# A graph attention layer on one Trainium2 core: block products and spread loads in batch 0, a store queue more in the tail, setup matmuls of 32 outputs

## The chip, the cores and the metric

The kernel runs on one core of one Trainium2 chip. The metric is the device time of one execution, in microseconds (us). Three executions of the kernel before took 587.0, 587.73 and 588.74 us; the median is 587.73. One more execution was recorded by the hardware profiler, and everything said of the inside of the kernel comes from that one. Engines go by their profile names: PE (TensorE matmul) and PEld (its weight loads), DVE (VectorE), ACT (ScalarE), POOL (GpSimd), SP (SyncE, which here only issues DMAs).

## The reference, cut to what matters

There are B = 16 batches of N = 512 tokens with F = 512 features (`v`, in the kernel `x`), one condition vector `q` per batch, and an integer mask `adj` of 11 labels per pair of tokens. Only the first 20 tokens (`NONGT`) serve as keys and values. Heads: 16 of 32 features. Everything is float32.

```
row_zero  = v.sum(-1) == 0
q_exp     = where(row_zero, 0, q)                      # per token
self_feat = concat([v, q_exp]) @ W_self.T + b_self
output    = self_feat
for d in range(2):                                     # two directions
    A    = (adj if d == 0 else adj^T)[:, :, :20]
    cond = A.sum(-1);  vb = A @ w_bias + b_bias
    kv   = self_feat[:, :20]
    qh, kh = self_feat @ Wq[d].T + bq[d], kv @ Wk[d].T + bk[d]      # 16 heads of 32
    aff  = where(cond > 0, qh . kh / sqrt(32), NEG) + vb
    out_t  = softmax(aff over the 20 keys) @ kv
    output = output + out_t @ Wout[d] + bout[d]
result = v + relu(output)
```

## The kernel before, in words

**Weights folded into the keys.** The queries are never computed. In a setup, for all 16 batches at once, the kernel forms the 20 key and value rows of each batch (`ps_kv`, L530 to L573: 16 matmuls of 128 outputs, `kv_terms`), the key rows kh (`key_rows`, L576: 32 matmuls of 128 outputs by 320 columns, L580), and multiplies them with Wq, so that a score is self_feat times one "g" column per head and key. This last step are 22 key bursts (`keys`, L659): a burst of matmuls (L668) into two pairs of banks, evicted by ACT (L683) and DVE (L685) into a stage `st`, which SP writes to DRAM (g1_d for batch 1, g_d for the later ones, L693 and L694) or copies to g0 for batch 0 (L690). While ACT and DVE evict a burst, PE is given other work by a plan written out by hand: `plan` (L713) has one word for each burst from the one at which the key rows are done, and each letter takes the next step of its kind: b biases, c bias scores, n row flags (ps_nz), v and w the values kv times Wout (ps_v, L643), s a quarter (8 matmuls) of half a block of self features.

**Self features.** For one batch, self_feat is a 512 x 512 by 512 x 492 product (the 20 key tokens come from the setup). Batch 0 computes it directly, in four blocks of 32 matmuls (ps_sf, L205, each of 32 outputs; four of them, on the four quarters of the array's columns, make one step). Three blocks are in the plan, the fourth stands in the loop at b = 0, nt = 1 (L867). Each is evicted by two DVE instructions (`self_copy`, L218). The later batches use seven products of half-size blocks instead of eight: sums of the weight blocks (`weight_sums`, L223) and of the x blocks (`x_sum`, L238) are made by POOL, each product (`product`, L249) is 16 matmuls of 32 outputs by 246 columns (L282) into the banks ps_a (two, kept accumulating through products 1, 6, 7 and 4), ps_d (product 2) and ps_c (5, then 3 on top), and DVE takes `partial` sums out of ps_a (L289) between products and adds them to ps_d and ps_c (`joined`, L299). A product on ps_a must wait until the partial before it has been read.

**The loop.** It runs over b (16 batches) and nt (4 tiles of 128 tokens); the order of every instruction is fixed by the program's text. In each step: `scores` (ps_s, L356, 128 matmul records), `weigh` on DVE (add the mask terms `full`, maximum, subtract: L370, L374, L378), `expo` on ACT (L383), `normal` of the previous tile (DVE sum and reciprocal L409 and L410, POOL multiply L411), `turn` (DVE transpose, L418). The products for batch b + 1 stand at nt = 2 (1, 2), nt = 3 (6, 7, 5), and at nt = 0, b + 1 (4, 3). `attend(b - 1)` (ps_o, L429) stands at nt = 2 of batch b: it multiplies the softmax weights with `vd`, a tile of value blocks; then `finish` (L438, L440), `residual` (POOL, L443) and `store` (L448). Mask terms of the next batch: `mask_mul` (ACT, L317), `mask_count`, `mask_sum` (DVE, L328), `mask_spread` (ACT, L337), `full_add` (POOL, L344). Row sums of x, which say where the q term is left out, are taken by ACT two batches ahead (`row_sum`, L169, from `xn`), turned into flags (`row_mask`) and loaded back over DRAM (`load_nz`).

**Value blocks.** bd_d in DRAM holds the values of all batches as blocks among zeros. SP clears it with one DMA of 2 MB (`clear_blocks`, L145) at b = 0, nt = 1, then copies the values vw_d into it with 12 DMAs from DRAM to DRAM (`blocks`, L162) at nt = 2, which wait for the clear. `load_values(b)` (L139) reads one batch of it into vd with four DMAs, which wait for the copies; for batch 0 this stands at nt = 3, ahead of the loads of x(2).

**Queues.** All loads and stores of the loop are issued by SP, in the order of the text. `behind(dma, ins)` (L95) gives a DMA a wait for an instruction of another engine, so that it isn't issued too early; SP then stands still until that instruction is done.

**The tail.** After the loop (L980 to L1014): `attend` of the last batch in two parts (three tiles, one tile), with the self features put into the banks by matmuls; `end` (DVE maximum, L996), a relu by ACT (L1006) with an add by POOL (L1009), and `send` (L998), four stores, all on SP. Just ahead, the last tile's softmax is done in two halves (`weigh_half`, `normal_half`, L385 and L396; L400 is the multiply, for the second half on DVE).

## Time and profile before

| What | Value |
|---|---|
| times of three executions | 587.0, 587.73, 588.74 us (median 587.73) |
| the profiled execution | 589.14 us, its span 587.3 us |
| granted TensorE clock in it | 0.995 |
| first key burst, first scores of batch 0 | 25.44 us, 91.15 us |
| first attend (batch 0's, in batch 1) | 132.13 us |
| batches 5 to 14 | 262 to 555 us |
| last DVE `end` done | 581.6 us |

The span is the time from the first to the last event that the profiler saw; the 1.8 us beside it are around the program. A row of a timeline gives start and length in us, the engine, the line of the kernel, the operation, the tile written and the tiles read, the shape, and the count in the group; brackets say how long the engine had been idle and what released it. The chain of waits follows the last instruction back, at each step to what released it or to the instruction before it on its engine; in order of time its rows are start, length and what it was. A float32 matmul appears as two records, so counts of PE records are twice those of the program.

### The profile page before, as it was taken

To read this page: it belongs to the slowest core of one execution; us is meant where nothing else is said; L and a number is where in the kernel's file an instruction comes from. 1 tells how busy PE (TensorE), PEld (TensorE's weight loads), DVE (VectorE), ACT (ScalarE), POOL (GpSimd) and SP (SyncE) were. 2 spreads that over 40 slices of the span, in tenths; PEclk is the share of its full clock that TensorE was granted. 3 is DMA by queue.
4 is the path that set the end of the run, shared out by engine and by line. 5 is a ranking of instruction groups with operands and counts; after the bars stand their busy time and mean duration, and the time that the engine had idled before them with its cause. 6 is when DMAs were issued, how large, how long until landed. Compare 5 with 4: busy or idle time off the path is not lost.

```text
span 587.3 us, 30302 instructions
## 1 busy us (share of the span) xinstructions
PE 575.0 (98%) x13180; PEld 436.8 (74%) x13180; DVE 491.2 (84%) x785; ACT 395.5 (67%) x1162; POOL 384.3 (65%) x351
## 2 busy tenths in 40 slices
PE   9999999999999999999999999999999999999993
PEld 6654547887778787877778787787878878787881
DVE  1485565889898989899999999998989898989895
ACT  1334534686877777878686868686877868776761
POOL 2406663548677685858586867776868686777774
PEclk9999999999999999999999999999999999999998
DMA  8999899857766675757676767675666766664403
GB/s 312 387 400 314 330 376 333 256 110 209 231 179 188 188 211 169 216 172 214 173 201 180 217 169 210 175 210 167 198 196 188 210 187 182 210 171 136 121 31 127
DMA packets 103221, 124.14 MB, mean 211 GB/s; under 512 B 21713, under 2 KB 71921, under 8 KB 101041
## 3 DMA queue, kind: packets, MB, share of 16 engines
q1 hardware_dynamic: 101840, 120.32, 66.3%
q8 instruction: 104, 1.70, 1.2%
q0 software_dynamic: 672, 1.36, 1.0%
q10 hardware_dynamic: 576, 0.53, 0.3%
q14 instruction: 29, 0.23, 0.1%
HBM read 82.30 MB, written 40.24 MB: 209 GB/s over the span
## 4 chain that ended last, share of the span: by engine, by line
PE 94%; DVE 3%; DMA 1%; issue 1%; ACT 0%; POOL 0%; SPq 0%; DVEq 0%; POOLq 0%; ACTq 0%
PE ps_s L356 44%; PE ps_a L282 17%; PE ps_c L282 9%; PE ps_o L429 6%; PE ps_d L282 4%; PE ps_v L643 3%; PE ps_k L580 3%; PE ps_sf L205 2%; DMA ws_q<-in_wsT 1%; PE ps_kv L531 1%; DVE o L438 0%; PE ps_nz L189 0%; DVE wt L418 0%; DVE ps_s L374 0%; DVE sm L409 0%
## 5 line engine op out<-in xcount | busy, mean ns | idle before, releaser
L356 PEld LDWEIGHTS ps_s<-g,sf 128*32 128x32 f32 x8192 | 263.3, 110 | 20.1 <-issue 12.2
L356 PE MATMUL ps_s<-g,sf 128*32 128x152 f32 x8192 | 276.7, 293 | 0.5 <-ACT st L683 0.5
L337 ACT COPY both<-add 32x80 f32<-32x80 f32 x512 | 130.9, 256 | 53.6 <-DVE add L328 47.6
L411 POOL TENSOR_TENSOR s<-s,sm 128x640 f32<-128x640 f32 x63 | 80.3, 1275 | 95.5 <-DVE sm L410 54.7
L344 POOL TENSOR_TENSOR full<-cq,both 128x640 f32<-128x640 f32 x64 | 100.2, 1565 | 28.5 <-issue 22.6
L317 ACT ACTIVATE prod<-adj,wb_sb 128x80 f32<-128x80 int32 x330 | 112.5, 432 | 0.8 <-DMA adj<-in_adj 0.8
L383 ACT ACTIVATE s<-s 128x640 f32<-128x640 f32 x63 | 46.5, 738 | 65.6 <-DVE s L378 65.3
L443 POOL TENSOR_TENSOR o<-o,x 128x512 f32<-128x512 f32 x60 | 76.0, 1288 | 0.0
L370 DVE TENSOR_TENSOR full<-ps_s,full 128x608 f32<-128x608 f32 x63 | 48.9, 777 | 29.7 <-PE ps_s L356 24.4
L409 DVE TENSOR_REDUCE sm<-s 128x32 f32<-128x640 f32 x63 | 50.9, 807 | 9.2 <-ACT s L383 8.9
L282 PE MATMUL ps_a<-t,ws_s 128*32 128x246 f32 x960 | 55.4, 370 | 0.0
L374 DVE TENSOR_REDUCE ps_s<-full 128x32 f32<-128x640 f32 x63 | 52.2, 828 | 2.2
L418 DVE STREAM_TRANSPOSE wt<-s 128x640 f32<-128x640 f32 x63 | 52.8, 839 | 0.1
L378 DVE TENSOR_TENSOR s<-full,ps_s 128x640 f32<-128x640 f32 x63 | 51.5, 818 | 1.1
L282 PEld LDWEIGHTS ps_a<-t,ws_s 128*32 128x32 f32 x960 | 31.5, 110 | 16.1
L328 DVE TENSOR_REDUCE add<-prod 128x80 f32<-128x960 f32 x32 | 36.8, 1150 | 6.1 <-ACT prod L317 4.3
L247 POOL TENSOR_TENSOR t<-x 128x492 f32<-128x492 f32 x30 | 34.4, 1148 | 10.2 <-DVE full L370 5.3
L429 PE MATMUL ps_o<-wt,vd 32*32 32x512 f32 (+5 forms) x816 | 37.8, 578 | 2.3 <-DVE wt L403 2.0
L440 ACT ACTIVATE o<-o,bo 128x512 f32<-128x512 f32 x60 | 38.3, 711 | 0.6 <-POOL biased L888 0.6
L438 DVE TENSOR_TENSOR o<-ps_o,sf 128x512 f32<-128x512 f32 x60 | 36.7, 668 | 0.0
L289 DVE SCALAR_TENSOR_TENSOR u<-nz,qw,ps_a 128x246 f32<-128x246 f32 x90 | 36.6, 449 | 0.0
L247 POOL TENSOR_TENSOR t<-x,t 128x492 f32<-128x492 f32 x30 | 34.4, 1147 | 1.9 <-DMA x<-in_xT 0.7
(238 smaller groups left out, 719.6 us busy)
## 6 DMA issues: line engine op xcount, KB each, us to landing
g_d<-st SPq DMA_DIRECT2D x16, 1064.0 KB, 5.8
g<-g_d SPq DMA_DIRECT2D x56, 304.0 KB, 3.6
out_T<-o SPq DMA_DIRECT2D x60, 256.0 KB, 3.5
x<-in_xT SPq DMA_DIRECT2D x56, 256.0 KB, 3.3
xn<-in_xn SPq DMA_DIRECT2D x52, 256.0 KB, 3.2
adj<-in_adj SPq DMA_DIRECT2D x56, 220.0 KB, 3.3
nz<-nz_d SPq DMA_DIRECT2D x14, 256.0 KB, 4.3
wk<-in_wkT SPq DMA_DIRECT2D x2, 1024.0 KB, 7.6
```

The source lines that it names most:

```text
L247: done["xsum"] = nc.gpsimd.tensor_sub(t, one, two)
L282: nc.tensor.matmul(to, lhs, x[:, k], start=start, stop=stop, skip_group_check=n != 2)
L317: nc.scalar.activation(p[:, :, l], a[:, :, l], AF.Identity, scale=wb_sb[:, l : l + 1])
L337: nc.scalar.copy(adds[b, h][bass.ts(a, R), :, g], add[r].rearrange("p (t m) -> p t m", t=2))
L344: done["full"] = nc.gpsimd.tensor_add(f, cqs[b].unsqueeze(1).to_broadcast(shape), adds[b, nt // 2][:, nt % 2].unsqueeze(2).to_broadcast(sh ...
L356: nc.tensor.matmul(bank[bass.ts(a, R), bass.ts(j, WD // HL)], sfs[b][:, k, bass.ds(nt * P + (2 * g + j) * R, R)], keys[:, k, a], start=(k ...
L374: nc.vector.tensor_reduce(mx, f, AX.X, ALU.max)
L378: done["weigh"] = nc.vector.tensor_sub(s, f, mx.unsqueeze(3).to_broadcast(full))
L411: done["normal"] = nc.gpsimd.tensor_mul(s, s, sm.unsqueeze(3).to_broadcast(full))
L418: nc.vector.transpose(wts[b][:, nt], s.rearrange("p a h m -> p (a h m)"))
L429: nc.tensor.matmul(banks[a][bass.ds(at // 2 * DH, n * DH)].rearrange("p (t n) -> p t n", n=32), vd[r, bass.ds(at * DH, n * DH)], wt[r, :, ...
L443: nc.gpsimd.tensor_add(o[:, c], o[:, c], xs[b][:, c])
```

## The change

Five things, told by the new program:

1. Batch 0 computes its self features by the seven products too. They are steps "p" of the plan, in the gaps of the last bursts, each with its partial or join on DVE right behind; nothing of it is left in the loop. The weight sums and the x sums of batch 0 (kept in a free slot of the self feature pool) are made by POOL at bursts 9 and 11. The values come earlier in the plan, the bursts 12 and 13 (counted from 0) have only a "w" behind them.
2. For all batches, `partial` writes into the block of self features itself and `joined` adds in place; the tile is made, and its first 20 columns are copied in, at nt = 2 rather than 3.
3. Loads in batch 0 are spread. The clear is eight DMAs of 256 KB, each behind an instruction of the loop, the last behind the POOL add `full_add(0, 2)`. The keys of batch 1 come in four parts, the masks of batch 1 in halves. `blocks()` stands after batch 1's last mask load and has 18 DMAs: its 12 copies and between them two key loads and four loads of xn(2). `load_values(0)` goes from b = 0, nt = 3 to b = 1, nt = 0, behind a `joined`, after the four loads of x(2). `row_sum(2)` goes to b = 1, nt = 0, on ACT ahead of that tile's mask spread and exponential, and `row_mask(2)` follows it.
4. In the tail, the POOL adds wait for the last multiply of the softmax (`done["half"]`), and two of the four stores are issued by ACT's queue.
5. In the setup, `kv_terms` and `key_rows` issue four matmuls of 32 outputs for each one of 128.

The diff, cut to its core:

```diff
-    def clear_blocks(zero):
-        nc.sync.dma_start(
-            bd_d.rearrange("c b r e i g -> (c b r) (e i g)").rearrange("(n p) w -> p n w", p=P),
-            zero.unsqueeze(1).to_broadcast([P, C * B * 32 // P, HL * 2 * DH]),
-        )
+    def clear_blocks(zero, n, ins):
+        half = bd_d[n // 2, n % 2 * (B // 2) : (n % 2 + 1) * (B // 2)]
+        behind(nc.sync.dma_start(
+            half.rearrange("b r e i g -> (b r) (e i g)").rearrange("(n p) w -> p n w", p=P),
+            zero.unsqueeze(1).to_broadcast([P, B * 16 // P, HL * 2 * DH]),
+        ), ins)
...
-                        nc.sync.dma_start(bb[:, r : r + hi - lo, e, i], vv[d, :, m : m + hi - lo, e])
+                        copies.append((bb[:, r : r + hi - lo, e, i], vv[d, :, m : m + hi - lo, e]))
+        for n, (to, of) in enumerate(copies):
+            nc.sync.dma_start(to, of)
+            if n in (2, 5):
+                load_keys(1, range(n // 3 + 2, n // 3 + 3))
+            if n in (7, 8, 9, 10):
+                load_xn(2, (n - 7) // 2, None, slice((n - 7) % 2, (n - 7) % 2 + 1))
...
-    def partial(b, n, f, l, to=None):
-        if to is None:
-            to = us[b, n] = xsum.tile([P, 2, HN], F32, tag=f"u{n}", name=f"u{b}_{n}")
+    def partial(b, f, l):
+        to = block(b, f, l)
...
             def kv_terms(fc, k):
-                nc.tensor.matmul(
-                    kv_ps[fc][:, :BM], ws_v[:, k, bass.ts(fc, P)], xkv[:, k],
-                    start=(k == 0), stop=(k == C - 1),
-                )
+                for a in range(HL):
+                    nc.tensor.matmul(
+                        kv_ps[fc][bass.ts(a, R), :BM], ws_v[:, k, bass.ds(fc * P + a * R, R)], xkv[:, k],
+                        start=(k == 0), stop=(k == C - 1),
+                    )
...
+            def block_product(n):
+                product(0, n)
+                f, args = {
+                    1: (partial, (0, 0, 0)), 2: (joined, (0, "d", 0, 0)), 6: (partial, (0, 0, 1)),
+                    7: (partial, (0, 1, 1)), 5: (joined, (0, "c", 1, 1)), 4: (partial, (0, 1, 0)),
+                    3: (joined, (0, "c", 0, 1)),
+                }[n]
+                f(*args)
...
-            plan = "bvv vv vv ccw vv ns ssss sssw vv vv ssss ssss vv vv nww ssss ssss".split()
+            plan = "bvv vvc vvc vvn vv vvw vv vv w w wn p p p p p p p".split()
...
+                if n == 9:
+                    row_sums(1)
+                    weight_sums()
                 if n == 11:
-                    row_sums(1)
-                if n == 13:
-                    weight_sums()
+                    new_self(0)
+                    for i in range(1, 5):
+                        x_sum(0, i)
...
                 if b == 0 and nt == 1:
-                    load_adj(1, 0)
-                    load_cq(1)
-                    clear_blocks(zero)
-                    load_adj(1, 1)
-                    load_xn(2, 0)
-                    load_xn(2, 1)
-                if b == 0 and nt == 2:
-                    blocks()
-                if nt == 2 and last or nt == 3 and b == 0:
+                    clear_blocks(zero, 2, done["xsum"])
+                if nt == 2 and last:
                     load_values(b)
...
                         mask_mul(b, 1)
+                        if b == 1:
+                            for j in range(4):
+                                row_sum(2, j)
                         product(b, 4)
...
-                        joined(b, 3, "c", 1, 1)
+                        joined(b, "c", 1, 1)
                         product(b, 3)
-                        if b > 1:
-                            load_values(b - 1, done["joined"])
+                        load_values(b - 1, done["joined"])
...
-                    if b == 0:
-                        self_feat(0, 1, 1)
...
                     full_add(b, 2)
+                    if b == 0:
+                        clear_blocks(zero, 7, done["full"])
...
-                    if b > 0 and more:
+                    if b == 0:
+                        load_keys(1, range(1, 2), done["sum"])
+                        load_adj(1, 1, done["normal"], slice(0, 1))
+                        load_adj(1, 1, None, slice(1, 2))
+                        blocks()
+                    elif more:
                         load_keys(b + 1, range(1), done["normal"])
...
-        send(0, 0, NT - 1)
+        send(nc.sync, 0, 0, NT - 1)
...
-            nc.gpsimd.tensor_add(o_last[:, n, ns], o_last[:, n, ns], xs[b][:, n, ns])
-        send(2, 0, NT - 1)
+            behind(nc.gpsimd.tensor_add(o_last[:, n, ns], o_last[:, n, ns], xs[b][:, n, ns]), done["half"])
+        send(nc.scalar, 2, 0, NT - 1)
         for q in range(4):
             end(NT - 1, NT, rest, q)
             if q % 2:
-                send(q - 1, NT - 1, NT)
+                send(nc.scalar if q == 1 else nc.sync, q - 1, NT - 1, NT)
```

`key_rows` is changed as `kv_terms` is; the other seven calls of `clear_blocks` stand at nt = 0 and 1 of batch 0.

114 lines of the change are left out of this document (53 added, 61 removed).

## The prediction

> **What bounds the kernel now.** I read the page first: the busy line and the chain of work that ended last, by engine.
>
> ```profile
> span 587.3 us, 30302 instructions
> ...
> PE 575.0 (98%) x13180; PEld 436.8 (74%) x13180; DVE 491.2 (84%) x785; ACT 395.5 (67%) x1162; POOL 384.3 (65%) x351
> ...
> PE 94%; DVE 3%; DMA 1%; issue 1%; ACT 0%; POOL 0%; SPq 0%; DVEq 0%; POOLq 0%; ACTq 0%
> ```
>
> TensorE is busy for 98% of the span and makes 94% of the chain. The view of windows says the same stage by stage; its columns are length, then busy time of PE, PEld, DVE, ACT and POOL, granted clock, DMA share and GB/s. Here stand the key bursts of the setup, the crowded part of batch 0, and batches 5 to 14.
>
> ```profile
> 38.79:91.15 52.36, 51.63 (x541) 24.88 (x541) 31.81 (x61) 24.50 (x57) 29.72 (x34) 1.00 0.94 347
> 107.21:132.13 24.92, 24.25 (x620) 20.75 (x619) 21.78 (x35) 19.57 (x64) 12.21 (x13) 1.00 0.64 149
> 262.00:555.00 293.00, 293.00 (x7504) 232.12 (x7500) 266.96 (x415) 224.17 (x676) 212.89 (x184) 1.00 0.65 187
> ```
>
> PE idles for 0 of 293 us in the loop, 0.7 of 52 in the bursts. So a microsecond of matmuls taken from PE is a microsecond off the end, unless a wait replaces it; and a wait of PE is never caught up, because no later stage has idle time to give back. The change touches setup, batches 0 and 1, and the tail; nothing of the 293 us moves. I therefore follow PE from the setup to its first attend (matmuls that read vd), then the tail.
>
> **Part 1: seven products for four blocks.** In the chain of waits in order of time (start, length, what; a matmul counts as two records) these are the pieces of the four blocks that go, and one product of the loop:
>
> ```profile
> 56.13 0.54 PE ps_sf L205 x8
> 58.06 1.73 PE ps_sf L205 x32
> 60.77 1.33 PE ps_sf L205 x24
> 70.32 1.73 PE ps_sf L205 x32
> 73.03 1.73 PE ps_sf L205 x32
> 85.45 1.86 PE ps_sf L205 x32
> 88.29 1.86 PE ps_sf L205 x32
> 95.49 3.45 PE ps_sf L205 x64
> 107.21 1.66 PE ps_a L282 x32
> ```
>
> Removed: 0.54 + 3 x 1.73 + 1.33 + 2 x 1.86 + 3.45 = 14.2 us. Added: seven products of 16 matmuls (32 records) and 246 columns. Back to back one is 1.66; between bursts the block of 236 columns took 1.73 where 236/246 x 1.66 gives 1.59, so switching costs 0.14: 7 x 1.80 = 12.6, less the 0.1 that the last saves. Gain **1.7 us** (12.5 for 14.2). The operands cost nothing on PE: weight sums and x sums are POOL work, and POOL is busy 29.72 of 52.36 us in the bursts; they are issued at bursts 9 and 11, and the first product that needs one comes six bursts later. The in-place partials are the same DVE instruction with another output, and the ACT copy of new_self only moves, on an engine that is busy 67% of the span.
>
> **Part 2: the new fill plan.** Between two key bursts PE does fill work while ACT and DVE evict the burst. From the same chain, with one eviction from the timeline:
>
> ```profile
> 56.66 0.71 PE ps_g(1, 3, 1, 0, 2)0_552 L668 x4
> ...
> 63.12 0.71 PE ps_g(2, 1, 0, 0, 2)0_635 L668 x4
> ...
> 66.44 0.33 PE ps_g(2, 1, 1, 1, 2)0_657 L668 x2
> ```
> ```profile
> 62.11 1.01 PE ps_v L643 x4
> ...
> 90.66 0.44 ACT st L683
> ...
> 91.15 4.34 PE ps_s L356 x128
> ```
> ```profile
> 67.52 1.17 DVE L685 TENSOR_SCALAR st<-ps_g(2, 1, 1, 1, 2)1_658 128x304 f32<-128x304 f32 x2 [1.72 <-PE ps_g(2, 1, 1, 1, 2)1_658 L668]
> ```
>
> Before, two bursts start badly (0.71 where 0.33 is usual), as their banks come free late: 2 x 0.37 = 0.75 gone. The 0.5 between the last burst and the scores (90.64 to 91.15) is filled by the last product: 0.5 gone. Against that, two gaps now hold only a "w", 1.01 us of PE, while an eviction takes 1.17 plus some 0.2 to start: 2 x 0.4 = 0.8 back; and a DVE join ahead of one eviction gives 0.25 back. Net gain **0.2** (between -0.6 and +1.2: no stall shrinks, or no new one comes).
>
> **Part 3: 32 outputs a matmul.**
>
> ```profile
> 16.51 8.93 PE ps_k L580 x32
> ...
> 26.42 2.35 PE ps_k L580 x8
> ```
>
> One 128-output matmul of 320 columns takes 8.93/16 = 0.558. Four of 32 outputs run beside each other: the product of the loop, four groups of four in 1.66 us, takes 0.415 a group for 246 columns, so 0.54 for 320. So 0.018 on each of 16 in a row, some 0.05 for each of the four groups that stand alone, and about 0.1 for the exposed kv groups: **0.4 gain**, bounds 0 (the four-fold issue takes what streaming gives) and 0.8.
>
> Sum to the first scores: 1.7 + 0.2 + 0.4 = 2.3. Before, they start at 91.15 with 3.45 of block still owed (94.6); now they start at **S = 92.3** with nothing owed.
>
> **Part 4: spread loads, and who waits for them.** From the chain, POOL's timeline, and the views of single lines (for a DMA line: issue time in ns as min/median/max, first and last issue):
>
> ```profile
> 109.29 0.67 issue
> ...
> 132.13 2.07 PE ps_o L429 x41
> ```
> ```profile
> 103.94 1.57 POOL L344 TENSOR_TENSOR full<-cq,both 128x640 f32<-128x640 f32 x1
> ```
> ```profile
> L162 SPq DMA_DIRECT2D bd_d<-vw_d x12: 613/674/1822, 108.5 to 119.4; - x12
> DMA to landing us min/median/max: 2.9/4.3/5.0
> ```
> ```profile
> L139 SPq DMA_DIRECT2D vd<-bd_d x4: 335/419/1817, 124.4 to 127.1; - x4
> DMA to landing us min/median/max: 1.7/3.2/3.4
> ```
> ```profile
> L111 SPq DMA_DIRECT2D xn<-in_xn x5: 376/471/1726, 103.2 to 139.5; - x5
> ```
>
> When PE wants vd: before, attend starts 132.1 - 91.15 = 41.0 after the first scores. Without the 3.45 block that is 37.5. The 0.67 stays: PE runs ahead of DVE, and product 6 must still wait for a partial to leave its bank; for one score half that now meets its partial I add 0.3. So S + 37.8 = **130.1**, 2.0 earlier than before.
>
> When vd is there: the copies into bd_d must follow the last clear. That is now issued behind a POOL mask add (103.94 + 1.57 = 105.5 before, 10.0 after the first scores end at 95.5, in a chain of DVE, ACT and POOL that the block of PE did not lengthen). Now the scores end at 96.6, the add at 106.6; the last clear of 256 KB lands some 3.5 later (an estimate, between the medians to landing of 3.2 here and 3.8 in part 5), at 110.1: 1.6 later than the copies began before. Then SP issues 18 DMAs where it issued 12, six loads of batch 1 and 2 lying between the copies. Before, first copy to last landing of vd was 127.1 + 1.7 - 108.5 = 20.3. One end: all as before, and six issues of 0.47 more: 110.1 + 20.3 + 2.8 = 133.2. Other end: none of the issues of 1.3 to 1.8 us that stood among the twelve: 11 x 0.67 + 6 x 0.47 = 10.2, landing 4.3, vd 4.4: 129.0. I take **132.4**, nearer to the end that is this queue's own record. The four loads of x(2), now ahead of vd on SP, lie in the wait for the copies' landing. So PE waits 132.4 - 130.1 = 2.3 us for vd, and its attend comes at 132.4 against 132.1: the setup's gain is gone by then, **+0.3**.
>
> A second wait sits at the same place: row_sum of batch 2 (four ACT passes) now stands on ACT ahead of the mask spread and exponential of batch 1, and waits for the fourth xn load, which SP issues among the last copies. By the same reckoning it holds batch 1's softmax, and through DVE product 6 of batch 2, to about the same point; it adds nothing while vd is as late, and keeps some of the loss if vd alone were early. Two things are hidden: adj, cq and key loads for batch 1 lie a stage or more ahead of their readers, and row_mask and nz of batch 2 follow later than before but are wanted a stage after.
>
> **Part 5: the tail.**
>
> ```profile
> 576.37 0.49 DVE L393 TENSOR_TENSOR s<-full,ps_s 128x320 f32<-128x320 f32 x1
> ...
> 578.20 0.95 DVE L400 TENSOR_TENSOR s<-s,sm 128x320 f32<-128x320 f32 x1
> ```
> ```profile
> 579.63 2.01 DVE L996 TENSOR_TENSOR o<-ps_o,x 128x384 f32<-128x384 f32 x6
> ```
> ```profile
> L999 SPq DMA_DIRECT2D out_T<-o x4: 383/433/1542, 580.6 to 583.3; - x4
> DMA to landing us min/median/max: 2.7/3.8/4.1
> ```
> ```profile
> 582.00:583.00 1.00, 0.00 (x0) 0.00 (x0) 0.00 (x0) 0.00 (x0) 0.00 (x0) 0.50 0.97 349
> ```
>
> The last multiply (L400, on the path) takes 0.95 beside POOL's residual adds, 0.49 is what its shape takes in L393; with the adds behind it, 0.46 goes. The adds then wait, but behind them on POOL and ACT stands only one store. [...] The last store, behind an issue of 1.54, was issued at 583.3 though DVE had ended at 581.6; two queues bring it to the end of DVE. But data already flow at 349 GB/s there, so little of that can be had: 0.3. [...] Tail **-0.8** (bounds -0.3, -1.3).
>
> **Sum.** +0.3 - 0.8 = -0.5: the profiled execution, 589.14 (span 587.3), would be 588.6. The median of the three timed runs, 587.73, lies 1.4 below the profiled one; the same step from it gives **587.2**.
>
> **Rivals.** (1) *Vd in time.* If the copies keep their median issue and vd lands by 130.1, PE never waits: -2.0 - 0.8 = -2.8, **584.9**. For it: of the 10.9 us between the first and last copy's issue only 11 x 0.67 = 7.4 is median issue, and the 2 MB clear no longer precedes them in one piece. Against: the six loads bring as many bytes into the same stretch. (2) *Slower: SP's long issues.* An issue that takes 1.8 where 0.67 is usual costs 1.15, and SP is in order, so each delays vd in full. Three more than before among the 18 give 132.4 + 3.4 = 135.8: +3.7 - 0.8 = +2.9, **590.6**. It decides (slower than no change) as soon as vd lands after 132.9, and beyond what can be told from 134.7 on. For it: one of four vd issues and one of five xn issues were of that length. Against: the median of the copies, 0.67, says that most were not. (3) *No use of the four-way split*: the small matmuls and short fills stall by what they should gain, 0.4 + 0.2 and up to 1 more. Since PE would wait for vd anyway, it only moves the wait: 587.2 to **588**.
>
> **How the numbers follow.** About 0.3% (1.8 us) is what a measurement of this kernel can tell from no change: below 586.0 is faster, above 589.5 slower. Forecast (the wait eats the setup's gain, the tail stays) 0.43 with rival 3 at 0.04; rival 1, 0.34; rival 2, 0.19. Of the forecast's own spread (585.4 to 589.2) 0.05 lies below 586.0, so faster 0.39, same 0.42, slower 0.19. The range goes from 584.3 (rival 1 with the best tail) to 590.2 (most of rival 2).
>
> **What would show it.** First scores at about 92.3, with no ps_sf pieces; bursts 12 and 13 after the first fill starting late; before the first ps_o in batch 1, a wait of PE of 1 to 4 us for a DMA of vd, and ACT's row sums waiting for xn; the last multiply at 0.5; the last store's issue at DVE's end. If PE goes from scores to attend with no wait, rival 1 is right; if vd lands after 134.7, rival 2. Wrong altogether would be a first score after 94, or a difference in the batches from 5 on.

## The result, and the profile after

The changed kernel takes **592.2 us** (median of 6, 591.46 to 593.66) where the kernel before takes 587.44 (median of 6, 586.28 to 588.74): the ratio is 1.0091, interval 1.0077 to 1.0104. It is slower by 4.8 us. The profiled execution took 593.66, its span 591.9 us; that of before 589.14 and 587.3. The page of the changed kernel, the same lines as before and the row of the granted clock:

```profile
span 591.9 us, 30856 instructions
...
PE 575.4 (97%) x13436; PEld 432.9 (73%) x13436; DVE 492.5 (83%) x788; ACT 395.6 (67%) x1162; POOL 388.9 (66%) x355
...
PEclk9999999997999999999999999999999999999997
...
PE 86%; DMA 4%; DVE 3%; SPq 3%; issue 1%; POOL 1%; ACT 1%; DVEq 0%; POOLq 0%; ACTq 0%
```

PE's part of the chain fell from 94 to 86%; DMA (4% for 1), SP's queue (3% for 0) and POOL (1% for 0) have taken its place. One slice of the clock inside the loop, the tenth (133 to 148 us), shows 7 where the others show 9 (the last slice, the tail, shows 7 too, and 8 before). Both point to one place. The chain in order of time, around the first attend:

```profile
91.94 1.80 PE ps_c L267 x32
93.73 1.80 PE ps_s L340 x55
...
106.38 1.53 POOL full L328
...
108.35 4.90 DMA bd_d<-zero
...
129.10 4.96 DMA bd_d<-vw_d
...
134.15 2.77 DMA vd<-bd_d
136.91 0.14 issue
137.05 4.47 PE ps_o L413 x48
141.52 4.62 PE ps_s L340 x128
```

It leaves PE at 95.5 and comes back at 137.05: mask add on POOL, last clear, copies, vd, attend. What PE itself waited for, and PE's columns in the windows there (length, PE, PEld, DVE, ACT, POOL, clock, DMA share, GB/s):

```profile
PE ps_o L413 <- DMA vd<-bd_d: 4.5, 1, 4.5
PE ps_o L413 <- DVE wt L387: 1.5, 1, 1.5
PE ps_s L340 <- DMA g<-g_d: 1.3, 1, 1.3
```
```profile
130.00:134.00 4.00, 2.51 (x80) 2.20 (x69) 0.59 (x2) 2.68 (x10) 0.25 (x1) 1.00 0.94 263
134.00:138.00 4.00, 0.95 (x17) 0.76 (x32) 1.97 (x4) 3.82 (x14) 1.74 (x2) 0.67 0.63 193
138.00:142.00 4.00, 4.00 (x60) 0.78 (x32) 2.68 (x4) 1.48 (x5) 4.00 (x4) 0.50 0.54 100
142.00:146.00 4.00, 4.00 (x128) 3.69 (x124) 3.13 (x6) 4.00 (x12) 1.06 (x2) 0.97 0.53 168
```

PE stands 4.5 us for vd (132.5 to 137.05), and then the clock is at half: the attend takes 4.47 where it takes 2.17, the scores behind it 4.62 for 4.27. The two spans, cut at the same events:

| Stretch | Before | After | Difference |
|---|---|---|---|
| to the first key burst (25.44, 26.57) | 25.4 | 26.6 | +1.1 |
| to the first scores, with the 3.45 of block still owed before | 69.2 | 67.2 | -2.0 |
| from there until PE comes to the attend (132.1, 132.5), without that block | 37.5 | 38.8 | +1.3 |
| wait for vd | 0 | 4.5 | +4.5 |
| first to second attend (163.57, 170.33) | 31.4 | 33.3 | +1.8 |
| second attend to the last DVE add of the loop (564.61, 570.16) | 401.0 | 399.8 | -1.2 |
| from there to the end | 22.7 | 21.7 | -0.95 |

The sum is +4.6. The first row is mostly the landing of the first large weight load (ws_q), at 10.28 for 9.32 in these two executions; over the executions of this study it lies between 9.1 and 11.2 for the same loads. The loop's -1.2 are three attends that took longer in the execution of before (2.62, 2.39 and 2.96 us for 2.17, at 194, 225 and 378 us), against one in the changed kernel (2.42); their cause is open.

### The profile page after: what moved, and what is told of

It reads as the page before. It is cut to its first block, busy times and chain, and to the rows that moved or that the text cites. A ratio compares the mean times of both kernels' runs of the same rounds, so it can differ in the third digit from the quotient of the medians.

```text
span 591.9 us, 30856 instructions
## 1 busy us (share of the span) xinstructions
PE 575.4 (97%) x13436; PEld 432.9 (73%) x13436; DVE 492.5 (83%) x788; ACT 395.6 (67%) x1162; POOL 388.9 (66%) x355
## 3 DMA queue, kind: packets, MB, share of 16 engines
q10 hardware_dynamic: 1120, 1.06, 0.5%
## 4 chain that ended last, share of the span: by engine, by line
PE 86%; DMA 4%; DVE 3%; SPq 3%; issue 1%; POOL 1%; ACT 1%; DVEq 0%; POOLq 0%; ACTq 0%
PE ps_s L340 40%; PE ps_a L267 17%; PE ps_c L267 8%; PE ps_o L413 6%; PE ps_d L267 4%; PE ps_k L566 3%; PE ps_v L629 3%; SPq L166 2%; DMA ws_q<-in_wsT 1%; DMA bd_d<-vw_d 1%; DMA bd_d<-zero 1%; PE ps_kv L516 1%; SPq L111 1%; DMA vd<-bd_d 0%; POOL s L395 0%
## 5 line engine op out<-in xcount | busy, mean ns | idle before, releaser
L340 PEld LDWEIGHTS ps_s<-g,sf 128*32 128x32 f32 x8192 | 263.1, 110 | 22.7 <-issue 13.7
L354 DVE TENSOR_TENSOR full<-ps_s,full 128x608 f32<-128x608 f32 x63 | 48.9, 776 | 25.0 <-PE ps_s L340 21.7
L393 DVE TENSOR_REDUCE sm<-s 128x32 f32<-128x640 f32 x63 | 50.8, 807 | 15.7 <-ACT s L367 15.6
L267 PE MATMUL ps_a<-t,ws_s 128*32 128x246 f32 x1024 | 59.3, 371 | 0.0
L273 DVE SCALAR_TENSOR_TENSOR sf<-nz,qw,ps_a 128x246 f32<-128x246 f32 x128 | 51.5, 443 | 0.7 <-PE ps_a L267 0.7
L267 PEld LDWEIGHTS ps_a<-t,ws_s 128*32 128x32 f32 x1024 | 33.8, 110 | 17.5 <-issue 1.0
L232 POOL TENSOR_TENSOR t<-x 128x492 f32<-128x492 f32 x32 | 36.8, 1150 | 9.1 <-DVE ps_s L358 7.1
L177 ACT ACTIVATE xn<-xn 128x512 f32<-128x512 f32 x56 | 34.4, 616 | 6.2 <-DMA xn<-in_xn 6.2
```

What stands on the lines that cost most here:

```text
L267: nc.tensor.matmul(to, lhs, x[:, k], start=start, stop=stop, skip_group_check=n != 2)
L273: done["partial"] = nc.vector.scalar_tensor_tensor(to[:, i], nzs[b][:, half(l)], qw[:, 2 * f + i, b : b + 1], parts[b, "a"][i][:, :HN], AL ...
L340: nc.tensor.matmul(bank[bass.ts(a, R), bass.ts(j, WD // HL)], sfs[b][:, k, bass.ds(nt * P + (2 * g + j) * R, R)], keys[:, k, a], start=(k ...
```

## The experiments

Ratios are to the kernel before on the same chip, five rounds each, with their 95% interval; the kernel before had medians of 586.9, 588.0, 588.4, 588.6 and 588.4 us in the five groups. Where a stop of PE is given, it is from the one profiled execution of that kernel. In e1, e3 and e9 that execution was the slowest of its group (588.76, 590.28 and 592.1 us, with medians of 586.92, 588.37 and 590.24), so a stop explains that execution; how long it was in the others isn't known.

**The loads of before under the rest of the change (e1).** All of part 3 undone.

```diff
-    def clear_blocks(zero, n, ins):
+    def clear_blocks(zero):
...
-                    clear_blocks(zero, 2, done["xsum"])
+                    load_adj(1, 0)
+                    load_cq(1)
+                    clear_blocks(zero)
+                    load_adj(1, 1)
+                    load_xn(2, 0)
+                    load_xn(2, 1)
+                if b == 0 and nt == 2:
+                    blocks()
+                if nt == 2 and last or nt == 3 and b == 0:
                     load_values(b)
```

> The changed kernel with the order of loads of the kernel before (one clear of 2 MB, twelve copies without loads between them, vd read at the end of batch 0, row sums of batch 2 in batch 0); products, tail and 32-output matmuls stay. Theory: the late vd is the whole loss, since in the changed trace PE waits 4.5 us for it and runs at half clock for some 5 us after. Then vd lands near 128.8 us, PE, which wants it near 130 to 131.5, doesn't wait, and the time is 1 to 2 us of setup and 0.9 us of tail under the kernel before: 584.5 to 585.6. Rival: the products in the setup are what costs (first scores at 93.7 us, not 92.3): the time stays above 589.

Ratio 0.9997 (0.9982 to 1.0011), 586.92 us. The 0.9% are back, and PE no longer waits for vd. But the gain of setup and tail, with which I had expected 584.5 to 585.6, isn't there. For the profiled execution the chain shows why, and the window behind it:

```profile
104.03 2.16 issue
106.19 4.83 PE ps_s L332 x89
```
```profile
106.00:108.00 2.00, 1.81 (x34) 1.56 (x37) 1.47 (x3) 2.00 (x7) 2.00 (x2) 0.61 1.09 387
```

In the middle of batch 0's scores PE stops for 2.16 us and waits for nothing that the profile shows ("issue"), with the DMA engines full; behind it the clock is 0.61.

**Tail alone (e2)**, on the kernel before.

```diff
-            nc.gpsimd.tensor_add(o_last[:, n, ns], o_last[:, n, ns], xs[b][:, n, ns])
-        send(2, 0, NT - 1)
+            behind(nc.gpsimd.tensor_add(o_last[:, n, ns], o_last[:, n, ns], xs[b][:, n, ns]), done["half"])
+        send(nc.scalar, 2, 0, NT - 1)
...
-                send(q - 1, NT - 1, NT)
+                send(nc.scalar if q == 1 else nc.sync, q - 1, NT - 1, NT)
```

> The kernel before with the new tail alone (POOL adds behind the last multiply, two stores issued by ACT). Theory: 0.8 to 1.0 us under the kernel before, as the prediction's fifth part and the distance from the last DVE add of the loop to the end of the span (22.7 us before, 21.7 in the changed trace) have it. Rival: the stores are bound by their data and only the multiply gains, 0.4 to 0.5 us.

Ratio 0.9986 (0.9973 to 1.0): 0.8 us by the ratio, 0.6 by the medians (586.36 and 586.94). The interval takes in both theories and reaches no change at all; in the trace the end, from the last DVE add of the loop, takes 21.9 us for 22.7. The last multiply in its timeline:

```profile
578.07 0.49 DVE L400 TENSOR_TENSOR s<-s,sm 128x320 f32<-128x320 f32 x1
```

**32 outputs alone (e3)**, on the kernel before.

```diff
-                nc.tensor.matmul(
-                    kv_ps[fc][:, :BM], ws_v[:, k, bass.ts(fc, P)], xkv[:, k],
+                for a in range(HL):
+                    nc.tensor.matmul(
+                        kv_ps[fc][bass.ts(a, R), :BM], ws_v[:, k, bass.ds(fc * P + a * R, R)], xkv[:, k],
```

> The kernel before with the matmuls of 32 outputs in the setup alone. Theory: 0.3 to 0.4 us under the kernel before (the row of 16 key matmuls was 8.93 us before and 8.84 in the changed trace, each group that stands alone 2.35 and 2.29). Rival: four times the instructions delay the start of the bursts, which begin 1.2 us later in the changed trace: 1 us above the kernel before. The alternative to that rival is that the 1.2 us are the loads of the weights, which landed 1.0 us later in that execution by chance.

Ratio 1.002 (1.0004 to 1.0036), 588.37 us: the time is about the rival's, its mechanism is not. The setup begins as before (first burst at 25.4), so the delay of the bursts isn't there; in the profiled execution the time goes in batch 0, at the first product for batch 1:

```profile
107.92 0.41 PE ps_a L282 x8
108.34 2.25 issue
110.58 2.66 PE ps_a L282 x24
```

That is the stop of the kernel before (0.67 us at 109.29, eight records into the next product), 32 records earlier, longer, and with the rest of the product at a slower clock (2.66 for 1.25; the windows from 110 to 112 and 112 to 114 have 0.67 and 0.50).

**PE kept busy while it waits (e4)**, on the changed kernel.

```diff
+                        if b == 1:
+                            for i in range(40):
+                                nc.tensor.matmul(
+                                    banks[i % 4][bass.ts(i % 4, R), :HN], ws_v[:, 0, :R],
+                                    xs[1][:, 0, half(0)], start=True, stop=True,
+                                )
                         attend(b - 1, banks)
```

> The changed kernel with 40 more matmuls that serve nothing ahead of batch 0's attend, in the banks that it is about to write, so that PE is busy (some 4.2 us) while it waits for vd. Theory: the wait itself stays, but the granted clock stays at 1.0 behind it, and the attend takes 2.2 us where it took 4.5 and the scores after it 4.3 where they took 4.6: 2.5 us under the changed kernel, near 589.7. Rival: the slow attend is the late landing of the last of vd's four loads, and the clock is a consequence of nothing here: 592 or, with work that runs past the landing, above.

590.6 us, ratio 1.0055 (1.0036 to 1.0074) where the changed kernel has 1.0091. Chain and window:

```profile
130.99 4.30 DMA vd<-bd_d
135.29 0.04 issue
135.33 2.73 PE ps_o L413 x47
138.06 4.27 PE ps_s L340 x128
```
```profile
134.00:138.00 4.00, 3.32 (x65) 1.04 (x54) 3.82 (x6) 2.38 (x8) 3.79 (x4) 1.00 0.64 95
```

The clock stays at 1.00, the scores take 4.27 again, and from the first attend to the second it is 31.1 us where the changed kernel takes 33.3. So some 2 us of the loss are the clock behind the wait, shown by matmuls that compute nothing.

**Sixteen matmuls of one column (e5), then ahead of the warm-up (e9)**, on the kernel before. Nothing else changes; they shift PE's instructions by 64 places.

```diff
             for _ in range(7):
                 nc.tensor.matmul(warm[:, :P], ones, ones, start=True, stop=True)
+            for _ in range(16):
+                nc.tensor.matmul(warm[:1, :1], ones[:, :1], ones[:, :1], start=True, stop=True)
```

> The kernel before with 16 more matmuls of one column in the warm-up ahead of the first weights, where PE waits anyway; nothing else. They shift every later PE instruction by 64 places (load and multiply, two passes each), which is what the 576 instructions of the 32-output matmuls come to against blocks of 256. Theory: PE's code comes in 16 KB loads of 256 instructions over the same DMA engines as the data; in the 32-output kernel PE stood 2.25 us at 108.3 us, in the middle of a product and with nothing that it waited for, while the clear and the loads filled the DMA engines, and then ran at half clock. If only the place of the block boundaries decides, this kernel has the same stop near 108 us and takes 1 to 2 us longer than the kernel before. Rival: the stop belongs to the 32-output matmuls or was chance of one execution; then this kernel takes the time of the kernel before.

Ratio 1.0069 (1.005 to 1.0088). The stop is there (2.52 us at the same matmul), but the first key burst also came 2.8 us later: the kv matmuls behind the small ones took 7.2 us for 4.7, which looks like a lower clock (argued from their length alone, 1.5 times; the half clock in the expectation of e9 is this argument too). So the second form, with 17 ahead of the warm-up and six warm-up matmuls:

> The kernel before with 17 matmuls of one column ahead of the warm-up and one warm-up matmul less: again 64 PE instructions more. In the run with the small matmuls behind the warm-up, PE's kv matmuls ran at half clock and the whole setup came 2.8 us later (first key burst at 28.2 us for 25.4), which mixed two effects. Theory: the clock is now warm, the setup starts as in the kernel before (within 0.6 us), and what is left is the stop of PE in batch 0 at the first product, 2.0 to 2.5 us where the kernel before has 0.67, and the clock lost behind it: 1 to 2.5 us over the kernel before. Rival: the stop was an effect of the late setup; then the time is that of the kernel before within 0.5 us.

Ratio 1.0029 (1.0008 to 1.0049). The first key burst comes 1.4 us later in the profiled execution, more than the 0.6 that I had allowed, partly by slower kv matmuls (5.4 us for 4.7) and partly by a wait for ws_q (0.8 us for 0.3). So not all of the 1.7 us that the ratio gives need be the stop. The stop is there:

```profile
109.09 0.42 PE ps_a L282 x7
109.51 2.69 issue
112.20 2.65 PE ps_a L282 x24
```

The same stop at the same matmul as in e3. What decides is where in PE's instructions it falls. The DMA rows of the page of before have a queue of kind "instruction":

```profile
q8 instruction: 104, 1.70, 1.2%
```

104 loads of 1.70 MB in all are 16 KB each; PE has 2 x 13180 = 26360 matmuls and weight loads, 253 for each of the 104. So this queue brings PE's code, in blocks; the page counts its packets, 1.2%, in the time of the same 16 DMA engines as the 66.3% of the largest data queue.

The traces show the blocks directly. Number all records of PE in a trace from 0 in order of their start, its waits for semaphores among them (26576 before, 255.5 for each of the 104 loads; 27093 in the changed kernel, 255.6 for each of its 106). The 20 traces have 30 waits of PE for "issue", of 0.24 to 2.69 us. 28 of them end at a record whose number, divided by 256, leaves 193, whatever the kernel; the other two (0.31 and 0.40 us, in e7 and e11) don't. And each of the 28 ends 1.2 to 1.6 us after a 16 KB transfer of this queue has ended. In the trace of before, one such transfer ends in each of the 103 stretches of 256 records between these places, and PE passes none of the places less than 1.3 us after it. From this I take it that PE goes on when its next block has come. 64 places are a quarter of a block: PE reaches the boundary one product (1.66 us) earlier, and stops 1.6 to 2.0 us longer.

**Clear in pieces with the old loads (e6).** As e1, with `clear_blocks(zero, n, ...)` at the eight places of the changed kernel.

```diff
-                    clear_blocks(zero)
+                    clear_blocks(zero, 2, done["xsum"])
...
+                        clear_blocks(zero, 7, done["full"])
```

> As the run with the old loads, but the clear is the eight pieces of the changed kernel, each behind its instruction of the loop; all other loads stay as in the kernel before. Theory: with the clear in pieces the DMA engines are not full for 20 us, PE's code arrives, and the stop of 2.2 us at 104 us and the half clock behind it (some 3 us in all) go; vd lands about as late as the last clear allows, near 132, against PE at 130 to 131: 584 to 585.5. Rival: the stop is something else, or the later clear makes vd later than PE by 2 us or more: 586.5 to 588.

Ratio 1.007 (1.0043 to 1.0097): the theory fell. PE's code still stops it, and PE waits 1.6 us for vd as well:

```profile
103.32 1.34 issue
...
115.00 1.73 issue
```

**Loads apart from the copies (e7)**, on the changed kernel.

```diff
-        for n, (to, of) in enumerate(copies):
+        for n in (2, 3):
+            load_keys(1, range(n, n + 1))
+        for to, of in copies:
             nc.sync.dma_start(to, of)
-            if n in (2, 5):
-                load_keys(1, range(n // 3 + 2, n // 3 + 3))
-            if n in (7, 8, 9, 10):
-                load_xn(2, (n - 7) // 2, None, slice((n - 7) % 2, (n - 7) % 2 + 1))
+        for h in range(2):
+            for j in range(2):
+                load_xn(2, h, None, slice(j, j + 1))
```

> The changed kernel, with the six loads taken out from among the twelve copies: the two key loads ahead of the copies, the four xn loads behind them. Theory: four issues fewer between the last clear and the last copy, 2.5 to 4 us with their share of long ones, so vd lands near 134 where it landed at 137.4, PE waits about 1.5 us less than 3 and keeps its clock: 3 to 4 us under the changed kernel, 588 to 589. Rival: the copies themselves (their issue by SP and the last clear's late landing) set vd: 591 or more.

Ratio 1.0107 (1.0087 to 1.0126), not better. The copies and vd in the views of their lines:

```profile
L168 SPq DMA_DIRECT2D bd_d<-vw_d x12: 612/724/1736, 113.0 to 123.7; - x12
```
```profile
L139 SPq DMA_DIRECT2D vd<-bd_d x4: 302/403/939, 130.0 to 132.9; - x4
DMA to landing us min/median/max: 3.5/5.2/5.9
```

The last copy is issued at 123.7 where it was 129.1, as expected; but eight loads (xn and x of batch 2) now stand between copies and vd, and vd, 32 KB a piece, takes 5.2 to land behind their 2 MB. PE waited 5.4 us. The six loads were only a part of the chain, and what stands just ahead of vd counts the same.

**Clear in the setup, copies early (e8)**, on the changed kernel.

```diff
+                if 11 < n < 20:
+                    clear_blocks(zero, n - 12, None)
...
-                        clear_blocks(zero, 0, done["weigh"])
-                        clear_blocks(zero, 1, done["exp"])
+                        blocks(range(4))
```

> The changed kernel with the clear moved to the bursts 12 to 19 of the setup (eight pieces, no waits), the copies in three groups of four in tiles 0 and 1 of batch 0, and vd of batch 0 read at the start of tile 2, ahead of the key and xn loads. Theory: vd lands before 125 us, PE doesn't wait for it at all, and the clear no longer meets PE's code loads of batch 0: the setup's and the tail's gain stay, 584 to 585.5. Rival: the clear in the setup holds back the stores of the keys, and with them the bursts, by about as much as 2 MB take (5 to 6 us), or the copies fill the DMA engines in tiles 0 and 1 and PE's code is late there: 587 or more.

Ratio 1.0081 (1.006 to 1.0102). The attend no longer waits; POOL does:

```profile
107.16 1.06 POOL L228 TENSOR_TENSOR t<-x 128x492 f32<-128x492 f32 x1 [13.71 <-DMA bd_d<-vw_d]
```

The x sums of batch 1 start at 107.2, as the last stores of the keys, behind the clear on SP, landed only at 106.7, and the sums seem to lie where the stages of the keys were (argued from those times, not tried by itself); PE waited 5.4 us through POOL and DVE.

**Spread loads alone (e10)**, on the kernel before: e1's edit the other way round.

```diff
-                    clear_blocks(zero)
+                    clear_blocks(zero, 2, done["xsum"])
...
-                        if b > 1:
-                            load_values(b - 1, done["joined"])
+                        load_values(b - 1, done["joined"])
```

> The kernel before with the spread loads of the change alone (clear in eight pieces, 18 DMAs in the copies, vd of batch 0 read in batch 1, row sums of batch 2 in batch 1). Theory: the last clear lands near 110, the copies' last near 131, vd near 134; PE, which wants vd at 131.5, waits 2.5 to 3.5 us and then runs at half clock for some us: 4 to 6 us over the kernel before. Rival: with PE later by the fourth block, the wait is mostly covered and the clear in pieces saves the stop of PE's code: 0 to 2 us over.

Ratio 1.0077 (1.006 to 1.0094), as the theory has it, with a longer wait than the 2.5 to 3.5 us that it had: without products, small matmuls or tail, part 3 alone makes the loss.

```profile
PE ps_o L437 <- DMA vd<-bd_d: 4.3, 1, 4.3
```

**Vd right behind the copies (e11)**: e7 with the xn loads ahead of the copies and `load_values(0)` at the old place.

```diff
-                        load_values(b - 1, done["joined"])
+                        if b > 1:
+                            load_values(b - 1, done["joined"])
...
-                if nt == 2 and last:
+                if nt == 2 and last or nt == 3 and b == 0:
                     load_values(b)
```

> The changed kernel with the xn loads and the two key loads ahead of the copies (while SP waits for the last clear anyway) and vd read right behind the copies, ahead of x(2). In the run with the loads apart the copies had landed at 128.3 us, but vd waited for eight loads of 2 MB in front of it and landed at 136.5. Theory: copies landed near 128 to 129, vd near 131.5, PE waits 0.5 to 1.5 us for it and keeps most of its clock: 586 to 588. Rival: the loads in front make the copies later, vd lands at 134 or later: 590 or more.

Ratio 1.0075 (1.0057 to 1.0093). The rival holds: with 1.6 MB more in front the copies take until 131.5 to issue (one issue took 4.8 us), and vd lands at 138.

**Batch 0's block first (e12)**: only its 128 KB are cleared and copied in batch 0, and the rest in batch 1.

```diff
+        clear_first(zero)
...
+                        blocks(True, range(3), done["weigh"])
...
+                        if b == 1:
+                            blocks(False, range(6))
```

> The changed kernel, with the value block of batch 0 alone cleared (128 KB) and copied first, its vd read in tile 2, and the clear and the copies for the other batches moved to batch 1, where nothing wants them before batch 2. Theory: vd lands before 120 us, 3.3 MB less go through the DMA engines before the first attend, PE neither waits for vd nor for its code: the gain of setup and tail stays, 584 to 586. Rival: what is moved to batch 1 (twelve copies, eight clears on SP) delays the loads of batch 2 behind them in SP's order, and PE waits there: 588 or more.

Ratio 1.0105 (1.0088 to 1.0123). The first half of the theory holds: vd waits for nothing, and the first attend starts at 129.9, 2.2 us ahead of the kernel before. Then the rival: the clears stand ahead of batch 3's xn on SP, ACT waits for them, and PE for DVE behind ACT:

```profile
144.35 0.63 ACT L188 ACTIVATE xn<-xn 128x512 f32<-128x512 f32 x1 [2.46 <-DMA xn<-in_xn]
```
```profile
PE ps_s L351 <- DVE sf L294: 2.9, 1, 2.9
```

**An own array for batches 0 to 2 (e13, e14)**, the large one cleared in batches 1 and 2 and filled in batch 3; e14 with the matmuls of 128 outputs.

```diff
+                if b in (1, 2):
+                    clear_blocks(zero, 4 * (b - 1) + nt, None)
+                if b == 3:
+                    blocks(False, range(3 * nt, 3 * nt + 3))
```

> The changed kernel with a small array of its own for the value blocks of batches 0 to 2: cleared (384 KB) and copied in batch 0, vd read in tile 2; the large array is cleared by one piece of 256 KB at the end of each tile of batches 1 and 2 and filled by three copies at the end of each tile of batch 3. Two more DMAs by POOL in the setup write the values of those batches apart. Theory: first attend near 130 as in the run with batch 0 first, no wait over 1 us in batches 1 to 4, the end 2.0 to 2.4 us of setup and 0.9 us of tail under the kernel before: ratio 0.995, 584.5 to 585.5 where the kernel before takes 587.7. Rival: wherever the 3.3 MB go they cost PE a wait, or PE's code stops elsewhere: ratio 1.0 or more.

> The same with the setup's matmuls of 128 outputs as in the kernel before. Theory: 0.3 us more than with 32 outputs, if neither meets a stop of PE's code (ratio 0.9955); its 64 instructions less against blocks of 256 put the block boundaries at other places, so a stop in one of the two and not in the other would show as 1 us or more. Rival: the 32-output matmuls cost time by themselves, and this kernel is the faster.

Ratios 1.0075 (1.0053 to 1.0097) and 1.0055 (1.0034 to 1.0076): the rival. First attend at 134.4 and 133.6, with a stop of PE's code (1.8 and 0.65 us near 100), and from batch 2's attend to batch 4's, around the copies, 6.2 and 3.0 us more than the 61.0 of two batches without a wait. I found no place for the 3.3 MB that costs less than the place of before.

**Shifts of PE's instructions (e15, e16, e17, e18).** The kernel of e1 with 17, 33 or 50 one-column matmuls ahead of a shorter warm-up (64, 128, 192 instructions more), and without the 32-output matmuls (576 fewer, which against blocks of 256 is 64 fewer, or 192 more). The first of them:

```diff
+            for _ in range(17):
+                nc.tensor.matmul(warm[:1, :1], ones[:, :1], ones[:, :1], start=True, stop=True)
-            for _ in range(7):
+            for _ in range(6):
                 nc.tensor.matmul(warm[:, :P], ones, ones, start=True, stop=True)
```

> The run with the old loads, with 17 matmuls of one column ahead of the warm-up and one warm-up matmul less (64 PE instructions more). Theory: the stop of 2.16 us at 104 us in that run belongs to one block boundary; shifted by a quarter of a block it falls elsewhere in the crowded stretch from 97 to 115 us, and its length changes by up to 2 us either way; the time follows it, between 584.5 (no stop) and 590 (a stop of 4), against 587.7 for the kernel before. Rival: the stop is set by the loads alone; the time is that of the run with the old loads, ratio 0.998 to 1.001.

> The same with 33 and one less (128 PE instructions more). Theory: as for 64, another length of stop, and at least one of the four shifts has a stop under 0.7 us and a ratio under 0.997, the gain of products and tail. Rival: ratio 0.998 to 1.001 in all four.

> The same with 50 and two less (192 PE instructions more). Theory and rival as for 128.

> The run with the old loads without the 32-output matmuls of the setup: products and tail alone, and 576 PE instructions less, 64 against blocks of 256. Theory: as for the shifts, and 0.3 us more for the larger matmuls. Rival: the 32-output matmuls are what lost the gain; then this kernel alone is under 0.997 and the three shifts are not.

| Kernel | Shift against 256 | Stops of PE in batch 0 | Ratio |
|---|---|---|---|
| e1 | 0 | 2.2 | 0.9997 (0.9982 to 1.0011) |
| e15 | 64 | 0.9 and 2.5 | 1.0 (0.9982 to 1.0017) |
| e16 | 128 | 1.1 and 0.7 (2.35 in batch 1) | 1.0011 (0.999 to 1.0032) |
| e17 | 192 | 0.9 and 0.7 | 0.9989 (0.9973 to 1.0005) |
| e18 | 192, no small matmuls | 0.4 and 0.5 | 0.9963 (0.9947 to 0.9979) |

The stops in the chains of e15, e17 and e18:

```profile
101.84 0.88 issue
...
107.22 2.52 issue
```
```profile
105.38 0.92 issue
...
112.05 0.74 issue
```
```profile
104.00 0.37 issue
...
110.33 0.54 issue
```

By the ratios alone the rival of e18 came true: e18 is under 0.997 and the three shifts are not. But e17 has the 32-output matmuls and e18 hasn't; they share the shift, and both stop at the same two places, under 1 us each, without loss of clock (e18 has 1.00 from 98 to 114, and the means of the two executions are 0.997 and 0.998), while the other shifts stop longer or elsewhere. e17, behind its pads, starts its first burst 1.4 us later than e18 (27.3 and 25.95), which is most of what lies between their ratios; from the first burst to the first scores both take 67.3 us. So the 32-output matmuls aren't seen to cost or bring anything (argued from one execution of each). The pads of e15 and e16 change the start of the setup too, so the table doesn't give the price of a shift by itself. e18, products and tail with the old loads and the old setup matmuls, is **faster than both kernels**: 585.68 us for 588.40.

## Why the prediction was wrong, point by point

The forecast was 587.2, within 0.3%; the kernel is 0.9% slower, outside the range, past the rival that was slower (590.6).

**The step that failed is the fourth part: "I take 132.4" for the landing of vd.** It landed at 137.4 (last issue and its landing below). The chain was right, link by link; the sizes weren't. Of the 5.0 us, 3.3 lie ahead of the first copy (issued at 113.4 for 110.1) and 1.7 behind it.

```profile
L166 SPq DMA_DIRECT2D bd_d<-vw_d x12: 536/616/1709, 113.4 to 129.1; - x12
DMA to landing us min/median/max: 3.6/4.1/5.0
```
```profile
L139 SPq DMA_DIRECT2D vd<-bd_d x4: 330/418/421, 134.1 to 135.4; - x4
DMA to landing us min/median/max: 2.0/2.4/2.8
```

- The mask add ended at 107.9 for 106.6: first scores at 93.7 for 92.3, of which some 1.0 is the late weight load of that execution.
- The last clear took 4.9 to land, not 3.5: three more clears and a key load had been issued in the 3 us ahead of it, and my 3.5 lay between medians of other transfers (3.2 and 3.8).
- First to last copy issued took 15.7; my two ends were 10.2 (medians) and 13.7 (the record of before with six short loads). The median, 0.62, was even shorter, but six of the 18 issues took 0.96 to 1.7, key and xn loads among them, where I had given the six loads 0.47 each. That is rival 2's mechanism, and it should have been in the forecast: long issues are frequent in the crowded stretch. Between 100 and 130 us 6 of SP's 25 issues took over 0.95 us before and 9 of 35 after; between 262 and 555 us it was 16 of 277 and 13 of 280.

**The clock was missing altogether.** A wait of 4.5 us cost some 6.5: the granted clock fell to 0.5 and the attend took twice its time, 4.47 for 2.17 (e4: some 2 us back with PE kept busy). The profile before has no long wait of PE in the loop, so no row showed it; but half clock at an idle PE stood in a row that I had quoted for something else (0.50 at 582 us, in the tail).

**"The 0.67 stays: PE runs ahead of DVE, and product 6 must still wait for a partial to leave its bank"** was a wrong reading. The stop is eight records into product 2, at no semaphore; it is PE's code (e3, e5, e9, and the count of records there). With all of the spread loads it is short (0.28 us at 99.2 in the changed kernel, none over 0.2 us in e10), a gain of theirs that I hadn't priced, though small beside the wait; the clear in pieces alone doesn't give it (e6).

**"adj, cq and key loads for batch 1 lie a stage or more ahead of their readers"** was wrong for the two key loads that stand among the copies: PE waited 1.3 us for the last of them (at 123.4), part of the 38.8 for 37.8. It cost nothing, since vd was later still.

**Right:** the products and the new plan, 1.7 + 0.2 forecast and about 2.0 measured to the first scores (a little of it from key rows that stand alone, 2.29 for 2.35); the tail, 0.8 forecast, 0.95 in the trace and 0.6 to 0.8 in e2, with the multiply at 0.49:

```profile
583.75 0.49 DVE L384 TENSOR_TENSOR s<-s,sm 128x320 f32<-128x320 f32 x1
```

ACT's row sums of batch 2 waited for xn as forecast (2.3, 1.7, 0.2 and 1.1 us for the four) and added nothing beside vd.

The 32 outputs gave nothing where I had 0.4 (the terms of that part, 16 x 0.018, 4 x 0.05 and 0.1, even add up to 0.6): the row of 16 took 8.84 for 8.93, and from the first q matmul to the key rows it was 7.3 us for 7.1. That the setup's gain is eaten by a wait for vd was the forecast; that the wait and its clock cost three times the gain was not.

What stays open: why the transfer of a block of code comes up to 2.7 us too late at some block ends and in time at most others (the trace shows when it ran, not when it was asked for), and whether spread loads could win with another order; beside the change's own, seven were tried (e6, e7, e8, e11 to e14) and none did.

## What to carry to other kernels

Follow each buffer that an in-order engine will want back to its first link, and compare its landing with the reader, link by link: a step freed on the bound engine makes that engine early, and what it then meets (a transfer, its own code) can cost more than the step, above all where an idle stretch also lowers the clock (0.50 behind the 4.5 us here). Reckon with long issues and landings in a crowded stretch, above all when more is put into it. And before a change of 1 us is judged, look whether a stop for "issue" moved: instructions of PE added or taken away ahead of it can shift it (e3, e5, e9, e15 to e18), and kernels that differ in little else lay 0.2 to 0.3% apart here, as much as the edits brought.

## What the runs showed of the hardware that I had not expected

Not only the wait of 4.5 us was followed by half clock (some 6.8 us of it from 135.4 on, as its windows add up, the last 1.7 us of the wait among them). Of six stops of PE over 2 us, five (2.16 to 2.69 us, in e1, e3, e5, e9 and e15) were followed by half clock for some 3.4 us, as the windows behind them add up (in e1 0.61 and 0.53 for 2 us each, in e3 0.67, 0.50 and 0.98); the sixth, in e16, was not, and neither were the 0.67 and 0.57 us of the kernel before (1.00 from 110 to 114 and from 151 to 155). The chain and the window of e16:

```profile
150.10 2.35 issue
```
```profile
152.00:154.00 2.00, 1.54 (x36) 1.19 (x40) 0.75 (x1) 1.92 (x8) 1.56 (x2) 1.00 1.02 306
```

PE's code came in loads of 16 KB, one for every 256 of PE's records (255.5 and 255.6 by the counts), and 28 of PE's 30 stops for "issue", of 0.24 to 2.69 us, ended at the same place of a count by 256. The six stops over 2 us lie in windows of 2 us with a DMA share of 1.00 to 1.07 (1.07 in e1, 1.06 in e3); shorter ones stand in emptier windows too, down to 0.4 (0.42 from 97 to 100 in the changed kernel).

SP's issue of a DMA took 0.37 us in the median in the loop and 0.6 between 100 and 130 us, but over 0.95 us for one in four there (15 of 60 in the two traces) and one in twenty in the loop (29 of 557), once 4.8 (e11). In both traces no issue of SP starts before the one ahead of it has ended, so a long one delays all that SP issues behind it.
